# A window attention stage in a four-layer kernel: 128 + 64 channel rows, values per pixel through DRAM, a respread schedule

## The chip, the cores and the metric

The kernel runs as one program on one core of a Trainium2 chip. The core has five engines with a queue of instructions each: TensorE (PE in the profile; PEld is its weight load), VectorE (DVE), ScalarE (ACT), GpSimd (POOL) and SyncE (SP), which here only issues DMAs. Each works through its own queue in order, and semaphores hold an instruction back until what it needs is there. The metric is device time of one execution in microseconds (us), lower is better.

## The reference

Four layers follow each other on an image batch x of 4 x 192 x 64 x 64 in float32: a deformable convolution with channel attention (layer 0), a non-local block (layer 1), overlapping window attention with a gated MLP (layer 2), and a masked depthwise convolution (layer 3). Only the attention of layer 2 is concerned here:

```python
y = _conv1x1(_ln_c(x, n1g, n1b), qkv_w, qkv_b)          # 192 -> 576 channels, each pixel
cols = _unfold(y, WS, STRIDE, PAD)                      # 8x8 windows, step 6, 3 zeros around
L = cols.shape[-1]                                      # 11 x 11 windows
win = cols.reshape(B, 3 * HEADS, ch, WS * WS, L).transpose(0, 4, 1, 3, 2)
q = win[:, :, :HEADS] * temp[None, None]                # 6 heads of 32 channels
k = win[:, :, HEADS:2 * HEADS]
v = win[:, :, 2 * HEADS:]
attn = jnp.einsum('blhic,blhjc->blhij', q, k) + bias[None, None]
e = jnp.exp(attn - jnp.max(attn, axis=-1, keepdims=True))
s = jnp.sum(e, axis=-1, keepdims=True)
s_img = _reverse(s, H, W)                               # overlapping windows added up
o_img = _reverse(jnp.einsum('blhij,blhjc->blhic', e, v), H, W).reshape(B, HEADS, ch, H, W)
out = (o_img / s_img[:, :, None]).reshape(B, C, H, W)
```

Note that the unfolding comes after the projection: outside the image q, k and v are zero, and a pixel in the overlap of windows has one value vector that up to four windows use.

## The kernel before

The program goes over the four images. For each it runs `layer1`, beside which the gathers of the next image's layer 0 are woven, then `windows` (the attention of layer 2), then `rest` (the remainder of layer 2, layer 3, and the next image's first MLP). The constants of all layers are loaded and folded by `constants()`, whose steps are taken between those of the first image's gathers; there the gain and shift of layer 2's first layer norm go into the weights `qkvT`, and its mean is taken out of them.

`windows` goes over 11 rows of windows (`wr`). Channels lie as two halves of 96 partitions. Two sets of strips `xs`, `qs`, `ks` hold 8 image rows (with the zeros around) of normalized input, queries and keys; a window row brings 6 new ones, and `shared` copies the 2 rows that it has in common with the row before, on POOL. The 97th partition of `xs` is a row of ones, which adds the bias in the projection. For a window row there are these parts:

- `load` fetches the new input rows (SP, one DMA); `norm` is a generator that can be run up to a named step: squares on ACT (SQUARE), variances on PE, then square, difference and maximum, logarithm and exponential for the inverse root on ACT and DVE (VARIANCE, INVERSE), then its spread to all partitions on PE (L392) and the multiplication on DVE (L1122).
- `project_rows` makes queries and keys of one half: two projections of two matmuls (L1150, L1151). A float32 matmul shows in the profile as two passes.
- `queries` and `inputs` lay `qs` and `xs` out by window on POOL (`by_window`).
- The 11 windows are taken in three groups of four. `scores` makes the scores of a group on PE (L1185), adds the position bias, takes the maximum and subtracts it on DVE (L1191, L1197, L1198). `exponentials` takes the exponential on ACT (L1203) and the sums of it on DVE (L1205, L1209).
- `turned` takes a pair of windows: it makes their values on PE from the laid out input (L1225) and copies them out on ACT (L1230), transposes the exponentials on PE (L1233) and copies them into `et` on ACT (L1237). `outputs` multiplies both into a strip in PSUM (L1253, L1261).
- `collect` copies the finished strip out, `inverses` takes the inverse of the sums (ACT), and `finish` spreads it on PE (L1298) and multiplies on DVE (L1299).

The order of all this is written out by hand under `tc.manual_schedule()`: the loop over `wr`, `g` and `pair` at the end of `windows` is the order in which each engine gets its work. In it the scores of a group are made one group ahead. In the first group of a row, each pair is followed by the projections of one half of the next row. Norms are made two rows ahead: SQUARE at the start of group 0, up to INVERSE at the end of group 1 and ahead of that group's exponentials, and the spread and multiplication at the start of group 2, ahead of its pairs. At the end of row 1, `load_image` fetches the whole image for `rest` with 16 DMAs on SP.

PSUM tiles with the tag "a" (projections, values, transposes, `finish`) share two buffers; the score tile, the norms' tile and the output strip have one each.

## Time and profile before

| what | us |
| --- | --- |
| median of 3 runs | 6399.53 (6394.88 to 6402.87) |
| the profiled execution, its own time | 6392.29 |
| its span, first to last instruction | 6390.5 |
| up to the first `windows` (first image's layers 0 and 1) | 1480 |
| first `windows` (1480 to 1748) | 268, PE busy 245.96 |
| first `rest` (1748 to 2190) | 442, PE busy 382.11 |
| one steady row of windows (1569.28 to 1592.32) | 23.04: PE busy 21.25, DVE 14.54, ACT 15.13, POOL 6.63 |

The boundaries are read from the chain of waits: the last matmul of layer 1 (L1041) ends near 1480, the first of `rest` (L1496) starts at 1748; the later images' `windows` lie at 2990, 4507 and 5747.

A line of the profile names the line of the kernel, engine, operation, then out<-in by the program's names, shapes as partitions x elements, and how often. In a group, the numbers after the bar are busy us in all and mean ns of one, and behind the second bar the engine's idle time just before, with what ended it. In order of time, a line begins with the start and the duration in us, and a bracket gives the idle time before it and what it waited for. `SPq` is the issue of a DMA on SP's queue. PEclk is the granted clock of TensorE, 1.00 at full speed.

### The profile page before, as it was taken

The page shows a single profiled execution, that of the slowest core. Times are in us where ns is not written, and L with a number is a line of the kernel's source. Part 1 is how long each engine was busy: PE and PEld are TensorE (multiplying, and loading weights), DVE is VectorE, ACT ScalarE, POOL GpSimd, SP SyncE. Part 2 cuts the span into 40 slices and gives each one's busy share as a digit, 9 for nine tenths or more (in the row PEclk, how much of TensorE's full clock was granted, in tenths as well). Part 3 has the DMA queues.
Part 4 walks back from the last instruction along what each step waited for, and adds up shares of the span by engine and source line. Part 5 has one row for each costly group of instructions (what it writes and reads, how often), then busy time and mean ns, then how long its engine had stood idle before and what let it go on. Part 6 is the DMA issues. An engine that isn't in the chain of part 4 may idle for free.

```text
span 6390.5 us, 106371 instructions
## 1 busy us (share of the span) xinstructions
PE 5900.9 (92%) x40528; PEld 4039.0 (63%) x40528; DVE 4612.9 (72%) x6850; ACT 3779.2 (59%) x6552; POOL 2111.3 (33%) x2293
## 2 busy tenths in 40 slices
PE   7888999999989899999988899999998989999897
PEld 4455588886544568887654458888654457776543
DVE  3864199985677669996676839998567867765667
ACT  3764388875654358885654438887565536545542
POOL 2763077752200047772210017775220000003200
PEclk8989999999989999999999999999998999999998
DMA  6995267751010267772110057775111010001000
GB/s 193 308 316 152 81 195 223 224 178 37 24 29 17 74 200 221 226 222 69 35 36 24 21 145 227 222 223 171 36 27 29 21 57 11 13 15 38 5 7 22
DMA packets 330117, 698.60 MB, mean 109 GB/s; under 512 B 59894, under 2 KB 216838, under 8 KB 328839
## 3 DMA queue, kind: packets, MB, share of 16 engines
q0 software_dynamic: 92736, 455.22, 22.0%
q1 hardware_dynamic: 236038, 235.78, 13.5%
q8 instruction: 321, 5.26, 0.3%
q14 instruction: 190, 1.55, 0.1%
q10 hardware_dynamic: 832, 0.79, 0.0%
HBM read 611.25 MB, written 78.87 MB: 108 GB/s over the span
## 4 chain that ended last, share of the span: by engine, by line
PE 63%; DVE 20%; ACT 5%; DMA 5%; issue 4%; SPq 2%; POOL 1%; POOLq 0%; DVEq 0%; ACTq 0%
PE y L1041 11%; PE s L973 10%; PE h L650 7%; DVE ha L1403 2%; PE h L1595 2%; PE qk L1150 2%; PE v L1225 2%; PE o L878 2%; PE qk L1151 2%; DMA ring<-table,idx 2%; DVE ga L1403 2%; PE po L538 2%; DVE gate L1403 2%; DVE row L639 1%; DVE top L980 1%
## 5 line engine op out<-in xcount | busy, mean ns | idle before, releaser
L632 POOL DMA_INDIRECT ring<-table,idx x1152 | 1671.1, 1451 | 946.0 <-DVE row L639 172.7
L973 PE MATMUL s<-ths,ph 96*128 96x256 f32 x4096 | 982.5, 381 | 6.4 <-ACT sc L975 4.0
L973 PEld LDWEIGHTS s<-ths,ph 96*128 96x128 f32 x4096 | 776.6, 191 | 131.1 <-ACT sc L975 6.3
L638 ACT ACTIVATE row<-ring,pos 128x384 f32<-128x384 f32 x1152 | 673.0, 609 | 240.4 <-DVE xo L643 147.2
L639 DVE SCALAR_TENSOR_TENSOR row<-ring,fr,row 128x384 f32<-128x384 f32 x1152 | 673.1, 611 | 111.2 <-ACT row L638 106.3
L1041 PE MATMUL y<-sc,gx 128*97 128x256 f32 x3008 | 716.4, 379 | 0.0
L1041 PEld LDWEIGHTS y<-sc,gx 128*97 128x97 f32 x3008 | 489.3, 164 | 127.5 <-issue 5.1
L642 ACT ACTIVATE xo<-row,pos 128x192 f32<-128x192 f32 x1152 | 485.5, 448 | 64.2 <-PE h L650 32.2
L643 DVE SCALAR_TENSOR_TENSOR xo<-row,fr,xo 128x192 f32<-128x192 f32 x1152 | 445.4, 411 | 41.5 <-ACT xo L642 39.3
L975 ACT COPY sc<-s 128x1024 f32<-128x1024 f32 x376 | 377.1, 1003 | 157.0 <-PE s L973 154.2
L1038 DVE TENSOR_TENSOR sc<-sc,mbs 128x1024 f32<-128x1024 f32 x376 | 453.0, 1217 | 19.8 <-ACT mbs L999 19.7
L1039 ACT ACTIVATE sc<-sc 128x1024 f32<-128x1024 f32 x376 | 393.3, 1053 | 75.2 <-DVE sc L1038 72.1
L980 DVE TENSOR_TENSOR top<-top,sc 128x1024 f32<-128x1024 f32 x282 | 344.0, 1220 | 128.6 <-ACT sc L975 128.4
L650 PE MATMUL h<-ti,xo 128*128 128x192 f32 x2304 | 434.6, 327 | 0.0
L650 PEld LDWEIGHTS h<-ti,xo 128*128 128x128 f32 x2304 | 388.8, 190 | 28.8 <-issue 8.2
L1205 DVE TENSOR_REDUCE eh<-ex 128x12 f32<-128x768 f32 x132 | 125.4, 950 | 317.1 <-ACT ex L1203 317.1
L1403 DVE SCALAR_TENSOR_TENSOR ga<-gate,v,ga 128x1024 f32<-128x1024 f32 x234 | 300.3, 1283 | 6.7
L650 PE MATMUL h<-kept,xo 128*128 128x192 f32 x960 | 239.2, 381 | 70.5 <-DVE xo L643 62.0
L1645 POOL COPY gate<-gate 128x192 f32<-128x192 f32 x12 | 4.2, 348 | 904.9 <-ACT gate L1638 904.9
L650 PEld LDWEIGHTS h<-kept,xo 128*128 128x128 f32 x960 | 169.7, 210 | 162.9 <-DVE xo L643 116.4
L855 PE MATMUL h<-d_l0m,fc 128*128 128x256 f32 x768 | 217.5, 427 | 59.1 <-ACT z L1601 22.5
L1041 PE MATMUL y<-se,gx 128*97 128x256 f32 x1088 | 261.1, 380 | 0.5 <-ACT yn L1047 0.5
(402 smaller groups left out, 11090.8 us busy)
## 6 DMA issues: line engine op xcount, KB each, us to landing
ti<-table SPq DMA_DIRECT2D x768, 48.0 KB
ring<-table,idx POOLq DMA_INDIRECT x1152
xnd<-xn SPq DMA_DIRECT2D x4, 3270.0 KB
xi<-in_x_dram SPq DMA_DIRECT2D x32, 384.0 KB
xk<-xd SPq DMA_DIRECT2D x32, 384.0 KB
xd<-xc SPq DMA_DIRECT2D x64, 192.0 KB
table<-tt SPq DMA_DIRECT2D x32, 384.0 KB
xc<-xd SPq DMA_DIRECT2D x60, 192.0 KB
```

Of the source, the lines that this page charges most:

```text
L632: nc.gpsimd.indirect_dma_start(out=gt.rearrange("p q r c -> p (q r c)"), out_offset=None, in_=corners, in_offset=bass.IndirectOffsetOnAxis ...
L638: nc.scalar.activation(row, gt[:, 0], AF.Copy, scale=pos[:, t, 9 + tap : 10 + tap])
L639: nc.vector.scalar_tensor_tensor(row, gt[:, 1], fr[:, t, 9 + tap : 10 + tap], row, ALU.mult, ALU.add)
L642: nc.scalar.activation(xo[:, j, :], row[:, 0, :], AF.Copy, scale=pos[:, t, tap : tap + 1])
L643: nc.vector.scalar_tensor_tensor(xo[:, j, :], row[:, 1, :], fr[:, t, tap : tap + 1], xo[:, j, :], ALU.mult, ALU.add)
L650: nc.tensor.matmul(acc[m // 2][:, bass.ts(m % 2, C)], lhsT=xo.rearrange("p j c -> p (j c)")[:, bass.ts(m, 128)], rhs=tt, start=t == 0 and ...
L973: nc.tensor.matmul(p[:, t, :], lhsT=ph[:, bass.ts(G * g + t, 128)], rhs=ths[i], start=True, stop=True)
L980: nc.vector.tensor_tensor(tops[i], tops[i], to, ALU.max)
L1038: nc.vector.tensor_tensor(ex, ex, mbs[i].unsqueeze(1).to_broadcast([128, G, QN]), ALU.add)
L1039: nc.scalar.activation(ex, ex, AF.Exp)
L1041: nc.tensor.matmul(py, lhsT=gx[:, G * g + t, :], rhs=ex[:, t, :], start=g == 0 and t == 0, stop=g == NG - 1 and t == G - 1,)
L1403: nc.vector.scalar_tensor_tensor(acc[:, b], src(tap, b), w[:, tap : tap + 1], acc[:, b], ALU.mult, ALU.add)
```

## The change

All of it concerns layer 2's attention.

- **Channels** lie as 128 and 64, the second block filled with zeros up to 128. `qkvT` is laid out so that its columns are 128 of q, 128 of k, then the last 64 of q beside the last 64 of k, then v. A row so has three projections (`t` = 0, 1, 2) of two matmuls with 128 rows and columns, where it had four with 96. The ones row is gone: the bias of q and k (`qkb`) is added by ACT as it writes them out, and the second block of q and k is written in two pieces of 64 partitions.
- **Strips** are the image rows 6 x wr to 6 x wr + 5, normalized into `xz` without zeros around, and not kept over rows. `qs` and `ks` hold 9 rows and share 3; `xs`, `xw` and `inputs` are gone.
- **Values** are made once per pixel: `values` multiplies 128 pixels at a time (three tiles a row where there were six pairs of windows), DVE adds the bias `vb`, and two DMAs write them to `values_dram`. `fetch` reads them back by window with 16 DMAs of 8 partitions each into `vw`, which `outputs` uses. The zeros around are written once, by POOL's DMAs for the first image.
- **Order**: the first and third projection and the values stay in group 0, the second projection goes to group 1. DVE's sums (`summed`) are taken after the next scores' bias, ahead of maximum and subtraction (`lowered`); in group 0 these two come after the first value tiles. The norm's spread and multiplication go behind the first pair of group 2, SQUARE to the end of group 2 a row earlier.
- **Loads** are two DMAs (128 and 64 partitions) into two fixed buffers whose lower part of the second block is set to zero once.
- **Constants**: the weights are loaded raw into a temporary tile (one DMA more) and scaled into `qkvT`; `qkb` and `vb` come from a few small matmuls; there is one step more. The gain, shift and temperature are also laid out as 128 and 64.

The diff, cut to its core:

```diff
+    values_dram = dram.tile([SW, STRIDE * (NWIN + 1), C], F32, tag="values", name="values")
...
             def load(wr, by=nc.sync):
+                n, at = strip(wr)
+                t = given[wr] = xrs[wr % 2]
+                lo, hi = split(t, n)
+                by.dma_start(out=lo, in_=x_flat[b % 2][0:M, at : at + n])
+                by.dma_start(out=hi[half(0)], in_=x_flat[b % 2][M:C, at : at + n])
...
+            if b == 0:
+                blank = s1.tile([128, 3 * C], F32, tag="blank", name="blank")
+                nc.gpsimd.memset(blank, 0.0)
+                for r in (0, 1, 2, SW - 1):
+                    nc.gpsimd.dma_start(out=values_dram[r, 0:SW], in_=blank[0:SW, 0:C])
+                inner = values_dram[PAD : PAD + H]
+                nc.gpsimd.dma_start(out=inner[:, 0:PAD, :], in_=blank[0:H].rearrange("p (w c) -> p w c", c=C))
+                nc.gpsimd.dma_start(out=inner[:, PAD + W, :], in_=blank[0:H, 0:C])
...
+                xz = xzs[wr] = sb.tile([M, 2, STRIDE * W], F32, tag="xz", name=f"xz_{name}")
+                nc.vector.tensor_tensor(xz[:, :, 0:n], src[:, :, 0:n], pb.unsqueeze(1).to_broadcast([M, 2, n]), ALU.mult)
...
+            def project_rows(wr, t):
+                qs, ks = sets[wr % 2]
+                n = strip(wr)[0]
+                rows, chans = slice(PAD, PAD + n // W), bass.ts(t, M)
+                p = ps2.tile([128, 512], F32, tag="a", name=f"qk_{b}_{wr}_{t}")[:, :n]
+                for k, part in enumerate(split(xzs[wr], n)):
+                    nc.tensor.matmul(p, lhsT=qkvT[:, k, chans], rhs=part, start=k == 0, stop=k == 1)
+                p = p.rearrange("p (r c) -> p r c", c=W)
+                temp = VW["l2_temp"]
+                if t == 1:
+                    nc.scalar.activation(ks[:, 0, rows, inside], p, AF.Identity, bias=qkb[:, 1:2])
+                    return
+                of, k = (half(0), 1) if t else (slice(0, M), 0)
+                nc.scalar.activation(
+                    qs[of, k, rows, inside], p[of], AF.Identity, bias=qkb[of, t : t + 1], scale=temp[of, k]
+                )
+                if t == 2:
+                    nc.scalar.activation(ks[half(0), 1, rows, inside], p[half(1)], AF.Identity, bias=qkb[half(0), 3:4])
+
+            def values(wr, part):
+                n = strip(wr)[0]
+                parts = split(xzs[wr], n)
+                tiles = [i for i in (2 * part, 2 * part + 1) if 128 * i < n]
...
+                    for j, i in enumerate(tiles):
+                        for k, of in enumerate(parts):
+                            nc.tensor.matmul(
+                                p[:, j, :], lhsT=of[:, bass.ts(i, 128)], rhs=qkvT[:, k, 2 * C :],
+                                start=k == 0, stop=k == 1,
+                            )
+                    nc.vector.tensor_tensor(
+                        vs[:, tiles[0] : tiles[-1] + 1, :], p, vb.unsqueeze(1).to_broadcast([128, len(tiles), C]), ALU.add
+                    )
+                if part == 0:
+                    return
+                m, r = n // 128, PAD + STRIDE * wr
+                to = values_dram[r : r + 2 * m, inside, :].rearrange("(i h) c k -> h c i k", h=2)
+                for h in range(2):
+                    nc.sync.dma_start(out=to[h], in_=vs[half(h), 0:m, :])
+
+            def fetch(wr):
+                vw = vws[wr] = sb.tile([128, (NWIN + 1) // 2, C], F32, tag="vw", name=f"vw_{b}_{wr}")
+                for i in range(2):
+                    n = (NWIN + 1 - i) // 2
+                    for r in range(WS):
+                        row = values_dram[STRIDE * wr + r, STRIDE * i : STRIDE * i + 2 * STRIDE * n]
+                        at = 64 * i + WS * r
+                        nc.sync.dma_start(
+                            out=vw[at : at + WS, 0:n, :], in_=row.rearrange("(n c) k -> c n k", n=n)[0:WS]
+                        )
...
                 for wr in range(NWIN):
                     for g in range(groups):
                         nxt = (wr, g + 1) if g + 1 < groups else (wr + 1, 0)
-                        if 0 < wr < NWIN - 2 and g == 0:
-                            norm(wr + 2, SQUARE)
                         if nxt[0] < NWIN:
-                            sc = scores(*nxt)
+                            sc, top = scores(*nxt)
+                        sums = summed(wr, g, ex)
+                        if nxt[0] < NWIN and (g > 0 or wr + 1 == NWIN):
+                            lowered(*nxt, sc, top)
                         if wr + 3 < NWIN and g == 1:
                             load(wr + 3)
-                        if wr + 2 < NWIN and g == 2:
-                            norm(wr + 2)
                         for pair in range(WG // 2):
-                            ops = turned(wr, g, pair, ex)
+                            ops = turned(wr, g, pair, (ex, sums))
                             if due is not None:
                                 outputs(*due)
                                 if g == 0 and pair == 0:
                                     collect(wr - 1)
                             due = ops
-                            if g == 0 and wr + 1 < NWIN:
-                                project_rows(wr + 1, pair)
+                            if wr + 1 < NWIN:
+                                if g == 0:
+                                    project_rows(wr + 1, 2 * pair)
+                                    values(wr + 1, pair)
+                                if g == 1 and pair == 0:
+                                    project_rows(wr + 1, 1)
+                                if g == 0 and pair == 0:
+                                    lowered(*nxt, sc, top)
...
+                            if wr + 2 < NWIN and g == 2 and pair == 0:
+                                norm(wr + 2)
                         if wr + 2 < NWIN and g == 1:
                             norm(wr + 2, INVERSE)
                         if nxt[0] < NWIN:
                             ex = exponentials(*nxt, sc)
-                        if g == 0 and wr + 1 < NWIN:
-                            for i in (1, 2):
-                                shared(wr + 1, i)
-                            queries(wr + 1)
-                            inputs(wr + 1)
-                        if g == 2 and wr + 2 < NWIN:
-                            shared(wr + 2, 0)
+                        if wr + 3 < NWIN and g == 2:
+                            norm(wr + 3, SQUARE)
+                        if wr + 1 < NWIN:
+                            if g == 0:
+                                shared(wr + 1, 0)
+                                queries(wr + 1)
+                            if g == 1:
+                                shared(wr + 1, 1)
+                                fetch(wr + 1)
```

## The prediction

> **What bounds the kernel now.** I read the sums over stretches first, then one steady row in order of time, then groups of instructions. The change works in four stretches, one for each image, in which `windows` runs. In the fences the columns after the stretch are busy us (and instructions) of PE, PEld, DVE, ACT and POOL, the granted clock, the share and the rate of DMA.
>
> ```profile
> span 6390.5 us, 106371 instructions
> 1480.00:1748.00 268.00, 245.96 (x3772) 161.75 (x3771) 160.97 (x234) 166.93 (x354) 76.94 (x207) 0.98 0.11 30
> 2990.00:3259.00 269.00, 246.50 (x3773) 162.37 (x3772) 160.64 (x234) 167.00 (x354) 76.95 (x207) 0.98 0.11 29
> 4507.00:4776.00 269.00, 246.47 (x3775) 162.29 (x3774) 160.93 (x234) 167.08 (x354) 76.92 (x207) 0.98 0.11 30
> 5747.00:6018.00 271.00, 246.89 (x3771) 162.69 (x3770) 161.36 (x235) 167.04 (x354) 82.27 (x209) 0.97 0.09 25
> ```
>
> TensorE is busy 92% of them, the other engines 62% or less. So the order on PE and its pauses set the time: 1077 us of 6390.5, 17%, and nothing outside can gain. A steady row takes 23.05 us (scores of its second group start at 1569.28, then at 1592.32), its three groups 9.75, 4.78 and 8.53. From start to start on PE: scores 0.73 each, a projection of four passes 1.35, a value block 0.68, three transposes 0.43, one pair's outputs 0.48, variances 0.9, spread 0.72, `finish` 0.69. That is 3 x 0.73 + 4 x 1.35 + 6 x (0.68 + 0.43 + 0.48) + 0.9 + 0.72 + 2 x 0.69 = 20.1 us; 2.9 are pauses, the longest here:
>
> ```profile
> 1584.95 0.21 DVE L402 TENSOR_SCALAR r_l2n<-r_l2n 128x96 f32<-128x96 f32 x1
> 1585.19 0.37 ACT L363 ACTIVATE r_l2n<-r_l2n,eps 128x96 f32<-128x96 f32 x1 [0.57 <-DVE r_l2n L402]
> 1585.60 0.28 ACT L364 ACTIVATE r_l2n<-r_l2n 128x96 f32<-128x96 f32 x1
> 1585.79 0.83 ACT L1203 ACTIVATE ex<-ex 128x768 f32<-128x768 f32 x1
> 1585.94 0.92 PE L392 MATMUL pb_l2n<-r_l2n,spread 128*96 128x96 f32 x8 [1.34 <-ACT r_l2n L364]
> ```
>
> PE waits 1.34 us for the norm's root; the exponential of the next group stands behind that root on ACT.
>
> **What it removes on PE.** Three projections in place of four: 1.35. Three value tiles of 128 pixels in place of six window pairs: 3 x 0.68 = 2.04. Filling to 128 rows costs nothing there: the spacing goes with the columns, and those stay 384 and 192. PE's work falls to 16.75 us a row.
>
> **What moves on the others**, by these groups (mean ns after the comma; last, DVE's idle time):
>
> ```profile
> L1205 DVE TENSOR_REDUCE eh<-ex 128x12 f32<-128x768 f32 x25 | 23.7, 949 | 60.2 <-ACT ex L1203 60.2
> L1191 DVE TENSOR_TENSOR ex<-s,bias 128x768 f32<-128x768 f32 x25 | 23.7, 948 | 0.0
> L1203 ACT ACTIVATE ex<-ex 128x768 f32<-128x768 f32 x25 | 20.9, 836 | 0.1
> L1230 ACT COPY vs<-v 128x192 f32<-128x192 f32 x41 | 13.1, 319 | 22.6 <-PE v L1225 22.5
> L1299 DVE TENSOR_TENSOR oi<-ot,rb 96x384 f32<-96x384 f32 x16 | 8.8, 547 | 3.9 <-PE rb L1298 3.9
> ```
>
> ACT loses six value copies (1.9 us a row) and writes projections in four pieces as before. DVE gains the bias of the values, 0.55 and 0.35 (as L1299's shapes). POOL loses the gather of `xw` and the shared rows of `xs`, 2.7 us of 6.6, off the path. DVE's sums now come behind the next scores' bias, so its 2.4 us of idle time a row for ACT go; but sums stand ahead of maximum and subtraction: from scores to exponential is 0.95 + 0.95 + 0.25 + 0.95 + 0.97 = 4.1 us on DVE, not 2.9. A row has 14.54 us of DVE and 15.13 of ACT before, 15.4 and 13.2 after, both below PE.
>
> **The pauses of the new row**, walked by hand in the new order with these durations. Group 0: PE 7.3 us, nothing late. Group 1: the second half of the third projection is written on ACT ahead of the exponential, 0.65 of pause before the transposes; work 4.85. On ACT then come copies, the projection moved here (0.58, it waits for PE), two inverses (1.04), copies, square, root, and the exponential ends 8.65 us after the group's start. PE has finished the next scores at 6.2 and needs it for the transposes: a pause of 2.4 us. The spread, moved behind them, no longer fills it. Group 2: PE's second `finish` needs the buffer that DVE's multiplication frees, which is behind sums, maximum and subtraction: 0.5. Together 16.75 + 3.7 = 20.45 us.
>
> Such a pause has a second price. In one row of the second stretch:
>
> ```profile
> 3204.70:3208.20 3.50, 3.50 (x69) 2.86 (x61) 2.65 (x4) 3.00 (x7) 2.32 (x8) 1.00 0.00 0
> 3208.20:3211.60 3.40, 2.02 (x90) 1.77 (x80) 1.87 (x4) 2.76 (x7) 0.00 (x0) 1.00 0.18 48
> 3211.60:3215.00 3.40, 3.40 (x27) 2.64 (x26) 3.29 (x5) 1.27 (x3) 0.00 (x0) 0.51 0.00 0
> 2085.22 2.93 PE L855 MATMUL h<-d_l0m,fc 128*128 128x256 f32 x6 [2.46 <-ACT gl L869]
> 2085.20:2088.70 3.50, 3.48 (x10) 2.38 (x12) 3.39 (x4) 0.33 (x1) 0.00 (x0) 0.51 0.02 5
> ```
>
> Around a pause of 1.38 us PE was busy 2.02 of 3.4 us, the clock was then 0.51 for 3.4 us, and this group took 10.13 us, not 8.53: 1.6 for one fall. A pause of 2.46 in another stage did the same. Most rows stay just above that edge now; with 2.4 us most would fall. I take four rows in five at 1.6 (bounds: none, and every row for two such stretches, 2.9): +1.3, a row of 21.75.
>
> The Trainium skill ("TensorE: Matmul & The Clock Gate", "HAM oscillation — how this bites in real kernels") asks only that PE have no idle gap above about 3.4 us. By that rule no row would fall and the total would be some 40 us lower; the rows above fell at 1.38 and 2.46, and I go by them.
>
> **The way through DRAM.** A row now has 2 stores, 2 loads and 16 fetches on SP, which issued one load. No row shows the fetch; the nearest, 8 partitions with 8 pieces each, is L302:
>
> ```profile
> L302 SPq DMA_DIRECT2D bias<-shifted x48: 685/685/812, 177.8 to 212.2; - x48
> 2113.20 2.06 DMA xd<-xa
> 611.85 2.91 DMA xa<-in_x_dram
> ```
>
> It went every 0.73 us (182.34, 183.07 in the chain); the medians of SP's other issues run from 0.30 (L1080) to 0.69, which is the range; single ones took up to 1.35, at L2027. From issue to the waiter a store took 2.0, a load 2.5 to 2.9. After the values' last add at 7.85 us of the row: stores at 7.9 and 8.5, landed 10.6, last fetch issued 10.6 + 15 x 0.73 = 21.6, landed 24.1. The first outputs of the next row want it at 21.75 + 4.8 = 26.5: hidden by 2.4 us, until a fetch costs 0.9. Twice in a stretch it isn't hidden:
> - Start: the last add at 1497.5 gives a landing at 1513.7; PE is there at 1509.5. Pause 4.2, the load of row 2 behind it holds up ACT's square, and the clock falls again: +6.5 (bounds 2 and 9).
> - `load_image` issues 16 DMAs (some 9 us on SP), which now follow row 1's long fetches and stand ahead of row 2's stores:
>
> ```profile
> 1527.00:1541.00 14.00, 12.90 (x220) 8.78 (x219) 6.66 (x10) 9.82 (x22) 5.34 (x19) 1.00 0.93 238
> ```
>
> They fill the DMA engines for 14 us. Counted from row 1's start: image from 22.3, engines free at 37, stores landed 38.6, fetches 52; wanted at 2 x 21.75 + 4.8 = 48.3. Pause 3.7 and a fall, +4.9 (bounds 0 and 9).
>
> The skill's "DMA: Bandwidth & Descriptors" ("Measured") calls transfers under 64 KB descriptor-dominated; these have 30 to 36 KB. Its figure for 64 KB, 0.95 us, taken as the issue step, would add some 25 us in all, an estimate.
>
> **Once.** The fold of the weights has one DMA more, a few little matmuls and DVE steps; L302 shows that SP's order is on the path there. On POOL six fills of zeros (0.68 each, as POOL's loads at L1080) and two more loads, mostly where POOL idles. +3 (0 to 10).
>
> **Sum.** Per stretch: rows 1 to 8, 8 x -1.3 = -10.4; rows 9 and 10, without norms and without the long pause, walked the same way 17.6 and 13 for 20.1 and 16: -5.5; start +6.5; image +4.9: -4.5. Four stretches -18, once +3: -15. The profiled execution took 6392.29 (span 6390.5), so 6377; the median of the runs shown is 7.2 higher, so **6384 us**.
>
> **Rivals.**
> - All that PE loses is gained (pauses stay 2.9, no falls): rows of 19.7, 8 x -3.35 = -26.8 in place of -10.4, total -81: 6319. For: PE is the bound by share. Against: DVE's longer way and ACT's order above.
> - Slower: each pause in group 2 costs two stretches of half clock (2.9). Rows then take 23.35, +0.3 x 8 in place of -10.4: total +33 to +40, 6437. It decides once a row loses over 2.6 us. For: after 1498.1 the clock stayed low for 10 us. Against: PE has work for 3.4 us after the pause.
> - Slower by SP: a fetch of 1.05 us makes the row 10.6 + 15.75 + 2.5 - 4.8 = 24.05; with start and image about +92, 6490. It decides from 0.98 us a fetch. Against: only single issues took as long.
>
> **How the numbers follow.** Forecast 0.45 (its own range 6350 to 6415), first rival 0.18, half clock 0.25, SP 0.08, something else 0.04. A measurement tells about 0.2%, 13 us. Faster: 0.25 of the forecast and the first rival, 0.43. Same: 0.17 of the forecast and the middle of the others, 0.23. Slower 0.34. Range 6300 to 6450: part of the first rival and the SP case stay out.
>
> **What would show it.** Right: PE's busy time in the stretches down by about 36 us each, transposes (L1233 of before) waiting 2.4 us for the exponential in group 2, clock 0.5 after many of them, rows near 21.7, pauses of some 4 us on outputs in rows 0 and 3 that a DMA of `vw` ends. Wrong: a fetch far from 0.73 us, rows near 19.7, or every row waiting for `vw`.

## The result and the profile after

The changed kernel took 6435.39 us (median of four runs, 6427.42 to 6444.96); the kernel before, beside it, 6397.20 (6393.62 to 6402.87). The ratio is 1.0055, with a 95% interval of 1.0039 to 1.0072: slower by 38 us, where the forecast was 15 us below the times shown. In a second comparison the ratio was 1.0038 (1.0022 to 1.0054).

From the page of the changed kernel: span, busy time by engine, and the group of transposes that answers to L1233 of before.

```profile
span 6431.4 us, 105494 instructions
PE 5832.6 (91%) x39860; PEld 4021.8 (63%) x39860; DVE 4645.4 (72%) x6899; ACT 3717.7 (58%) x6288; POOL 1979.4 (31%) x1989
...
L1325 PE MATMUL t<-ident,ex 128*128 128x128 f32 x792 | 156.6, 313 | 151.3 <-ACT ex L1300 151.3
```

PE issues 668 matmuls fewer and is busy 68 us less, and yet the span is 41 us longer. The last line says where PE stood: 151 us ahead of transposes, all of it waiting for the exponential on ACT. The four stretches, from the first filler matmul of `windows` to the first matmul behind it (columns as in the prediction):

```profile
1495.50:1764.30 268.80, 218.18 (x3594) 150.20 (x3593) 168.22 (x244) 151.82 (x288) 56.52 (x143) 0.92 0.26 65
3017.60:3296.90 279.30, 229.00 (x3593) 156.75 (x3593) 168.01 (x244) 151.82 (x288) 52.75 (x136) 0.87 0.24 61
4546.50:4822.70 276.20, 225.95 (x3594) 154.69 (x3593) 168.50 (x244) 151.90 (x288) 52.79 (x136) 0.88 0.24 62
5800.30:6065.10 264.80, 220.01 (x3544) 152.41 (x3543) 167.53 (x240) 149.33 (x285) 50.86 (x128) 0.89 0.23 59
```

Cut the same way, the stretches of before take 268.3, 269.3, 268.6 and 264.5. So the stretches give +18.5 us of the 41, at a clock of 0.87 to 0.92 where before had 0.97 to 0.98. The other 22.5 lie outside: the first gather ends 20.8 us later.

A steady row in order of time, start and duration in us, the pause of group 2 (the instructions of ACT and DVE that decide it, and PE's next):

```profile
3225.38 0.52 ACT L1384 ACTIVATE rs<-ot 6x384 f32<-6x384 f32 x1
3225.93 0.52 ACT L1385 ACTIVATE rs<-rs 6x384 f32<-6x384 f32 x1
3226.16 0.80 PE L1279 MATMUL s<-ks,qw 32*64 32x64 f32 x48
3226.46 0.97 ACT L1329 COPY et<-t 64x384 f32<-64x384 f32 x2
3227.45 0.25 ACT L435 ACTIVATE r_l2n<-pv_l2n 128x96 f32<-128x96 f32 x1
3227.73 0.26 DVE L436 TENSOR_TENSOR r_l2n<-pv_l2n,r_l2n 128x96 f32<-128x96 f32 x1 [2.35 <-ACT r_l2n L435]
3228.27 0.38 ACT L398 ACTIVATE r_l2n<-r_l2n,eps 128x96 f32<-128x96 f32 x1 [0.57 <-DVE r_l2n L437]
3228.68 0.28 ACT L399 ACTIVATE r_l2n<-r_l2n 128x96 f32<-128x96 f32 x1
3228.87 0.83 ACT L1300 ACTIVATE ex<-ex 128x768 f32<-128x768 f32 x1
3229.75 0.47 PE L1325 MATMUL t<-ident,ex 128*128 128x128 f32 x1 [2.80 <-ACT ex L1300]
```

The scores of the next group are done at 3226.96, and PE's next work is the transposes at 3229.75. The exponential they need was lowered on DVE by 3225.4, but stands on ACT behind the inverses, two copies and the root. The sums over stretches of 3.4 us around that pause:

```profile
3222.50:3225.90 3.40, 3.40 (x71) 2.33 (x71) 2.82 (x4) 2.07 (x4) 0.00 (x0) 1.00 0.69 172
3225.90:3229.30 3.40, 1.05 (x63) 0.77 (x54) 1.33 (x3) 2.72 (x7) 0.00 (x0) 1.00 0.39 104
3229.30:3232.70 3.40, 2.95 (x21) 1.80 (x22) 2.90 (x4) 1.35 (x3) 0.00 (x0) 0.50 0.11 28
3232.70:3236.10 3.40, 3.40 (x28) 2.67 (x26) 1.56 (x3) 0.69 (x2) 0.00 (x0) 0.50 0.00 0
3236.10:3239.60 3.50, 3.50 (x72) 2.09 (x70) 2.31 (x3) 2.28 (x5) 0.00 (x0) 1.00 0.02 5
```

PE is busy 1.05 of 3.4 us, and the granted clock is then 0.50 for two such stretches. Rows (from the scores of one row's third group to those of the next) take 21.1 us where the clock did not fall, 22.5 with one stretch at half clock and 23.7 to 23.9 with two. In these four stretches the clock falls 11, 14, 12 and 11 times; before it was 1, 2, 1 and 2.

### The profile page after: what moved, and what is told of

Same layout as the page of the kernel before. It is cut to its first block, busy times and chain, and to the rows that moved or that the text cites. A ratio compares the mean times of both kernels' runs of the same rounds, so it can differ in the third digit from the quotient of the medians.

```text
span 6431.4 us, 105494 instructions
## 1 busy us (share of the span) xinstructions
PE 5832.6 (91%) x39860; PEld 4021.8 (63%) x39860; DVE 4645.4 (72%) x6899; ACT 3717.7 (58%) x6288; POOL 1979.4 (31%) x1989
## 3 DMA queue, kind: packets, MB, share of 16 engines
q0 software_dynamic: 93264, 455.82, 21.9%
## 4 chain that ended last, share of the span: by engine, by line
PE 62%; DVE 19%; ACT 8%; DMA 5%; issue 4%; SPq 1%; POOL 1%; DVEq 0%; ACTq 0%; POOLq 0%
PE y L1076 11%; PE s L1008 10%; PE h L685 6%; PE qk L1203 3%; PE po L573 2%; PE h L1699 2%; DVE ha L1507 2%; DMA ring<-table,idx 2%; PE o L913 2%; DVE ga L1507 2%; PE t L1325 2%; DVE row L674 2%; DVE gate L1507 1%; PE o L1345 1%; DVE top L1015 1%
## 5 line engine op out<-in xcount | busy, mean ns | idle before, releaser
L1329 ACT COPY et<-t 64x384 f32<-64x384 f32 x484 | 231.4, 478 | 253.7 <-PE t L1325 248.7
L1325 PE MATMUL t<-ident,ex 128*128 128x128 f32 x792 | 156.6, 313 | 151.3 <-ACT ex L1300 151.3
L890 PE MATMUL h<-d_l0m,fc 128*128 128x256 f32 x768 | 213.3, 420 | 59.1 <-ACT z L1705 22.5
```

## The experiments

They were made in four sittings, in which the kernel before took 6394 to 6579 us, so each ratio is to its runs in the same sitting. The sum of the four stretches comes from each profile; "start" runs from the first filler to the first scores in stretches 1 to 3. A single stretch of the same kernel can differ by 10 us between two profiles (the changed kernel's first: 268.8 and 278.4), so small differences in the sums say little.

| run | ratio to before (95%) | four stretches, us | start, us | steady rows, us |
|---|---|---|---|---|
| before, twice | 1; 1.0012 (0.9994 to 1.0030) | 1071; 1071 | 18.0; 18.2 | 23.05 |
| changed, twice | 1.0055; 1.0038 | 1089; 1092 | 31.2 | 21.1 to 23.9 |
| x_warm | 0.9932 (0.9904 to 0.9960) | 1033 | 31.1 | 21.03 |
| x_spread | 0.9943 (0.9922 to 0.9963) | 1033 | 30.8 | 20.4, some 22 to 23.3 |
| x_exp | 0.9884 (0.9851 to 0.9917) | 1006 | 31.2 | 19.98 |
| x_expinv | 0.9863 (0.9828 to 0.9898) | 998 | 31.1 | 19.88 |
| x_load | 0.9990 (0.9965 to 1.0015) | 1071 | 19.4 | 21.1 to 23.9 |
| x_raw | 1.0022 (1.0003 to 1.0041) | 1087 | 30.4 | 21.1 to 23.9 |
| x_best2 | 0.9773 (0.9747 to 0.9800) | 930 | 19.4 | 18.76 |
| x_fetch2 | 1.1813 (1.1775 to 1.1852) | 2268 | 31.2 | 48 |
| x_fetchd | 1.0224 (1.0200 to 1.0248) | 1210 | 24.6 | 22.5 to 25.4 |
| b_spread | 1.0018 (0.9993 to 1.0043) | 1095 | 18.2 | 23.1, 24.7 |
| b_exp | 1.0039 (1.0018 to 1.0060) | 1102 | 18.1 | 23.2, 24.6 |
| b_best | 1.0018 (1.0007 to 1.0030) | 1079 | 18.2 | 23.17 |

**x_warm: the pause filled.**

```diff
                             sc, top = scores(*nxt)
+                        if wr + 2 < NWIN and g == 2:
+                            keep_warm(pvs[wr + 2][:, 256:512], 4)
```

> The changed kernel with four matmuls of 256 columns into an unused part of the variances' bank (an estimate from the 0.73 us that 384 columns take: 4 x 0.49 = 1.95 us) put on PE between the scores and the transposes of group 2, where PE now stands still for 2.8 us. It adds work and takes no wait away. Theory 'clock': the pause costs little itself beyond its 2.8 us; what makes rows differ (21.1 us without a fall, 22.5 with one stretch at half clock, 23.9 with two) are the falls after it. With the fillers the clock stays at 1.0 in rows 3 to 8 and every row takes 21.1: per stretch -6, -14, -12.5, -12.5, in all -45, some 6390 us. Rival 'chain': rows are set by the way from scores to exponential on DVE and ACT, PE's slower clock lies beside it, and the fillers gain under 10 us: 6425 to 6435.

Work was added, and the stretches became 56 to 59 us shorter than those of the changed kernel's two profiles, where 45 were expected. All rows from the third to the eighth take 21.03 us. The same place in the row:

```profile
3321.80:3325.20 3.40, 2.20 (x100) 1.78 (x98) 1.06 (x2) 2.80 (x6) 0.00 (x0) 1.00 0.16 43
3325.20:3328.60 3.40, 3.37 (x29) 2.60 (x30) 2.78 (x5) 2.29 (x5) 0.00 (x0) 1.00 0.37 96
3328.60:3332.00 3.40, 3.40 (x78) 2.34 (x76) 2.80 (x5) 1.22 (x2) 0.00 (x0) 1.00 0.01 4
```

The fillers themselves waited 1.24 us for the reader of their bank, and a pause of that length leaves PE busy 2.2 of 3.4 us: the clock stays at 1.00. "Clock" holds, "chain" falls: the half clock after the pause, not the pause alone, makes rows long.

**x_spread: one part of the change undone.** The spread of the root goes back ahead of the pairs.

```diff
+                        if wr + 2 < NWIN and g == 2:
+                            norm(wr + 2)
                         for pair in range(WG // 2):
...
-                            if wr + 2 < NWIN and g == 2 and pair == 0:
-                                norm(wr + 2)
```

> The changed kernel with only the spread of the norm's root put back ahead of the pairs of group 2, where it was before the change. PE then waits for the root itself, 2.1 us after the scores by the trace, runs the spread (1.1 us) and has the exponential ready right after it. Theory 'cover': the later place of the spread is a loss of the change by itself, about 0.7 us a row in work that no longer fills the pause, and the falls with it, since a pause of 2.1 us with more work around it makes the clock fall less: rows of 20.2 to 20.5 without a fall, some falls left, ratio 0.990 to 0.998. Rival 'same pause': the clock falls as before and the spread only changes places with the transposes, rows of 22.5 to 23.9, ratio 1.002 to 1.007.

"Cover" holds: 56 to 59 us less in the stretches than with the spread later, ratio 0.9943. In a row of it:

```profile
3285.42 0.80 PE L1279 MATMUL s<-ks,qw 32*64 32x64 f32 x48
3287.94 0.28 ACT L399 ACTIVATE r_l2n<-r_l2n 128x96 f32<-128x96 f32 x1
3288.13 0.83 ACT L1300 ACTIVATE ex<-ex 128x768 f32<-128x768 f32 x1
3288.27 2.02 PE L427 MATMUL pb_l2n<-r_l2n,spread 128*128 128x96 f32 x8 [2.05 <-ACT r_l2n L399]
3290.09 0.85 PE L1325 MATMUL t<-ident,ex 128*128 128x128 f32 x3
```

PE starts again 2.05 us after the scores, and the spread covers the exponential. This row still fell (the spread takes 2.02 us at half clock); most others did not and took 20.4. With the exponential where the change left it on ACT, undoing the later place of the spread is enough to turn the loss into a gain. It is not the only way: x_warm and x_exp keep that place and gain as well.

**x_exp and x_expinv: the order on ACT.**

```diff
+                        if nxt[0] < NWIN:
+                            ex = exponentials(*nxt, sc)
                         if wr + 2 < NWIN and g == 1:
                             norm(wr + 2, INVERSE)
-                        if nxt[0] < NWIN:
-                            ex = exponentials(*nxt, sc)
```

In x_expinv, `inverses(wr - 1)` also goes from the first pair of group 1 to behind that exponential.

> The changed kernel with the exponential of the next scores put ahead of the norm's root (the last step of the norm in group 1) on ACT; nothing else moves. In the trace ACT is ready with the copies 1.3 us before the exponential starts, and its scores are lowered on DVE 3.4 us before. Theory 'order on ACT': the pause of 2.8 us in group 2 shrinks to 1.5, which lies at the length that mostly did not make the clock fall before: rows of 19.8 to 20.5, 26 rows with some 2.5 us less, 6360 to 6375 us. Rival 'DVE': the exponential waits for the lowering on DVE, so moving it gains under 0.3 us a row: 6425 to 6435.

> As the kernel before this one, and the two inverses (0.52 us each) of the finished row also moved behind the exponential on ACT. Theory 'order on ACT': the pause shrinks to about 0.5 us, no falls, rows of 18.8 to 19.5: 6320 to 6345 us. Rival 'late root': the norm's root and the inverses then end some 2.3 us after the exponential, and PE waits for them at the finish or the spread of group 2 instead, so that the row is no shorter than with the exponential alone moved: 6360 to 6375.

The same place in a row of x_exp:

```profile
3240.51 0.96 DVE L1296 TENSOR_TENSOR ex<-ex,mx 128x768 f32<-128x768 f32 x1
3243.54 0.84 ACT L1300 ACTIVATE ex<-ex 128x768 f32<-128x768 f32 x1
3244.44 0.55 PE L1325 MATMUL t<-ident,ex 128*128 128x128 f32 x3 [1.39 <-ACT ex L1300]
```

The exponential was held up by its place on ACT, not by DVE: the pause is 1.39 us for 2.80, rows take 19.98 (19.8 to 20.5 was expected), the steady ones without a fall, and the stretches are 83 to 86 us shorter. The ratio of 0.9884 is a larger gain than the 0.994 to 0.997 that 6360 to 6375 us would be. Moving the inverses too gave 0.1 us a row where 0.5 to 1.2 were expected. The root then ended later, and the spread waited 0.65 us for it: "late root" holds.

**x_load: the start.**

```diff
-                xr = s1.tile([M, 2, STRIDE * W], F32, tag=f"xr{j}", name=f"xr{j}_{b}")
+                xr = sb.tile([M, 2, STRIDE * W], F32, tag="xr", name=f"xr{j}_{b}")
                 nc.gpsimd.memset(xr[half(1), 1, :], 0.0)
                 xrs.append(xr)
-            load(0, nc.gpsimd)
-            load(1, nc.gpsimd)
+                load(j, nc.gpsimd)
```

> The changed kernel with the two tiles of loaded rows taken from the first pool, where they lay before the change, and each tile's zeros and load in turn. In the trace of the changed kernel the zero fill of the first tile waits on POOL until 1504.08 for the store of the last attention result, and the two first loads stand behind it; before, the load was there at 1480. Theory 'place in memory': the tile shares its memory with the stored tile; without that the first row's variances start at about 1501 in place of 1507.6, each start of the stretch is 5 to 7 us shorter, -20 to -28 in all: 6407 to 6415 us. Rival 'values first': the start is long because all values and projections of row 0 now come ahead of the first scores at half clock, and the load is not what sets it: under 8 us, 6427 to 6435.

The start of the changed kernel, in order of time:

```profile
1501.73 0.31 SPq L1050 DMA_DIRECT2D xd<-xc  x1
1504.08 0.77 POOL L1124 MEMSET xr<- 64x384 f32 x2 [86.92 <-DMA xd<-xc]
1504.80 0.59 POOL L1118 DMA_DIRECT2D xr<-xd  x1
1507.61 1.03 PE L1170 MATMUL pv_l2n<-xr,mean_all 128*32 128x96 f32 x16 [6.43 <-DMA xr<-xd]
...
1510.79 3.43 DVE L437 TENSOR_SCALAR r_l2n<-r_l2n 128x96 f32<-128x96 f32 x1
...
1513.64 0.51 POOL L1154 MEMSET rs<- 128x512 f32 x1
...
1514.26 0.37 ACT L398 ACTIVATE r_l2n<-r_l2n,eps 128x96 f32<-128x96 f32 x1 [3.79 <-DVE r_l2n L437]
```

The zero fill waits for the store of `xc`, the load stands behind it, and PE stands still for 6.43 us. With the tile in the other pool:

```profile
1583.02 0.85 ACT L1161 ACTIVATE sq_l2n<-xr 128x768 f32<-128x768 f32 x1
1588.19 0.54 PE L1168 MATMUL pv_l2n<-xr,mean_all 128*32 128x96 f32 x16
1589.70 0.92 DVE L437 TENSOR_SCALAR r_l2n<-r_l2n 128x96 f32<-128x96 f32 x1
1601.97 0.80 PE L1277 MATMUL s<-ks,qw 32*64 32x64 f32 x48
```

The first row is there at once, and a start takes 19.4 us for 31.2: twice what was expected: a step of 3.43 us on DVE also shrinks to 0.92, and the clock stays at 1.00. Against 18.0 before, a start is still 1.4 us longer, with values and projections ahead of the scores. "Place in memory" holds for three stretches. The four together became only 18 to 21 us shorter, the low end of what was expected: rows 1 to 8 took 181.7 us for 178.2 and 178.8 in the changed kernel's two profiles, with more rows of 23.9, and the fourth stretch gained nothing at its start (19.1 for 19.8; 12.2 before). There no store holds up the load; L437 takes 5.51 us in x_load and 5.55 in the changed kernel where its like took 0.91 before. The ratio of 0.999 is below the 1.002 to 1.003 that 6407 to 6415 us would be; the stretches explain about half of what this run gains on the changed kernel, the rest was not followed.

**r_before, r_after and x_raw: outside the stretches.** x_raw releases the raw weights of the fold only after the tables of relative positions are loaded:

```diff
-        raws.close()
...
+        raws.close()
         v48 = late("v48", a["v48"])
```

> The kernel before, unchanged, profiled on the chip on which the next runs are made, so that the stages outside the four stretches can be set against each other on one chip. Both theories expect a ratio of 1.000; the stage up to the first normed rows (551.4 us in the first profile) may differ by tens of us from chip to chip.

> The changed kernel, unchanged, on the same chip. Of the 41 us between the two first profiles 19 lie in the four stretches and 22 outside, nearly all of these before 572 us (20.8 there). Theory 'fold': the outside part belongs to the change (the longer fold of the weights ahead of the chain of little DMAs on SP), and the end of the first gather is again 15 to 21 us later than in the kernel before on this chip. Rival 'chip': it is scatter of the gather, and the end of the first gather differs by less than 8 us either way.

> The changed kernel with the raw weights of the fold held until after the tables of relative positions are loaded; only the place in memory of the tile 'shifted' changes. In the trace of the changed kernel the first DMA of 'shifted' starts on SP at 175.30 us, when the last matmuls of the fold have read the raw weights whose place it takes; before it started at 168.19. Theory 'fold blocks SP': the chain of 48 little DMAs and the load of xi behind it start at 163 to 166 us in place of 175 and the first gather ends 8 to 14 us earlier than in the unchanged kernel: 6420 to 6428 us by the first chip's numbers. Rival 'work': the gather is late because of more work on PE and DVE in the fold, and the earlier DMAs gain under 4 us.

The last matmul of the first gather starts at 550.5 and 571.3 us in the first two profiles, at 607.4 and 612.4 in the second two: +20.8 and +5.0. The second is the rival's "less than 8", so most of the 20.8 is not shown to belong to the change. In x_raw the first DMA of `shifted` starts at 169.6 for 176.5 (163 to 166 was expected) and the gather's last matmul at 604.1 for 612.4: 8.3 us earlier, the low end of "fold blocks SP"; in x_best2, which has this edit too, at 606.7. The ratios 1.0022 and 1.0038 have overlapping intervals. The other profiles show how far such numbers scatter, since the edits inside `windows` do not touch this gather. With the constants of before it ends at 609.3 and 616.6 (b_spread, b_exp), in the same sitting with those of the change at 614.6 and 617.3 (x_spread, x_fetch2); in the last sitting at 559.3 (b_best) and 565.2 (x_fetchd). So in three sittings the change costs 3 to 6 us here, one kernel differs by up to 7 from profile to profile, and x_raw's 8.3 is hardly more than that.

**x_fetch2 and x_fetchd: are the fetches hidden?** Each fetch twice, first into the same tile, then into one that nobody reads:

```diff
-                        nc.sync.dma_start(
-                            out=vw[at : at + WS, 0:n, :], ...
+                        for t in (vw, vx):
+                            nc.sync.dma_start(
+                                out=t[at : at + WS, 0:n, :], ...
```

> The changed kernel with every fetch of the values issued twice (32 DMAs on SP a row in place of 16, the same data). In the trace 16 fetches are issued in 5.6 to 8.2 us, 0.35 to 0.5 us each, not the 0.73 that the prediction took from another shape; in steady rows they are issued some 9 us ahead of the first outputs that need them, in row 0 about 1 us ahead. Theory 'hidden': steady rows keep their length, only the first outputs of a stretch wait, by 5 to 7 us: +20 to +28 us, ratio 1.008 to 1.010. Rival 'SP bounds': every row waits for its values with 6 to 8 us more, over +100 us, ratio 1.02 or more.

> The changed kernel with every fetch issued a second time into a tile of its own that nobody reads: 16 DMAs more a row on SP (5.6 to 8.2 us by the trace) and twice the data, no wait between the two. Theory 'hidden': steady rows keep their 21.1 to 23.9 us, since 16 fetches are issued some 9 us ahead of the outputs that need them; only the first outputs of a stretch, which had about 1 us to spare, wait 5 to 7 us more: +20 to +30 us, ratio 1.007 to 1.011. Rival 'SP bounds': all rows become longer by 2 us or more, +70 us, ratio 1.015 or more.

x_fetch2 measured something else. What SP waited for, and who waited for the tile (us, times):

```profile
  DMA vw<-values: 1313.8, 51
...
  PE o L1346: 1112.8, 44
```

The second copy of each fetch waited for the landing of the first, since both write the same place. It shows what values cost that are late in every row (25 us a row), not what 16 issues cost. In x_fetchd, with no such wait, 32 issues take 15 us a row for 6.2, and steady rows from the fifth to the eighth stay at 22.5 to 25.4, within 2 us of the changed kernel's: hidden there. But row 0 takes 23 to 26 us for about 19, and row 2, with the image's load in it, 30 to 34 for 21 to 23. The ratio is twice what was expected and the stretches grew by about 120 us where 20 to 30 were expected: by these numbers alone the rival (1.015 or more, +70 us) would hold. Its mechanism does not, since it wanted every row longer: from the fifth to the eighth, four rows take 94.2 us on average for 93.7. What grew is row 0 (by 6 us), row 2 (by 10) and rows 9 and 10 with the end (by 6), and the way to row 0's third group (by 5), although the first scores came 6.6 us earlier, which says that the extra tile also moved others in memory. "Hidden" holds for steady rows alone.

**b_spread, b_exp and b_best: the same order in the kernel before.**

```diff
 b_spread: norm(wr + 2) behind finish(wr - 1, pair) of the first pair of group 2
 b_exp:    also exponentials(*nxt, sc) ahead of norm(wr + 2, INVERSE)
 b_best:   also inverses(wr - 1) at the end of group 0
```

> The kernel before with one part of the change alone: the spread of the root after the first pair of group 2 in place of ahead of the pairs. There a value block of 0.68 us still stands between scores and transposes, and the exponential is ready 0.7 us after the root. Theory 'cover': PE's pause only goes from the spread (1.34 us) to the transposes (about 1.4), rows stay within 0.3 us of 23.05, ratio 0.999 to 1.003. Rival 'falls': the clock, which in rows of before just held, now falls in most rows: rows of 24.5, ratio 1.005 to 1.007.

> The kernel before with the spread after the first pair and the exponential ahead of the norm's root, as in the changed kernel with that order. Tells what the order on ACT is worth without the new layout. Theory 'order on ACT': the exponential is ready at 1585.56 for 1586.62, the pause of PE before the transposes shrinks from 1.3 to 0.3 us, the root is still in time for the spread behind them: rows of 21.9 to 22.3, 8 a stretch, some -30 us, ratio 0.994 to 0.996; the rest of what the changed kernel with this order gains over before (rows of 20.0) is then the new layout's. Rival: the root is late for the spread by as much as the exponential was, rows of 22.9 to 23.1, ratio 0.999 to 1.001.

> The kernel before with the whole mended order: the exponential ahead of the norm's root, the inverses at the end of group 0, the spread after the first pair. Theory 'layout': the kernel before has 20.1 us of PE work a row and 2.9 of pauses, so the order can give at most some 1.5 us a row; rows of 21.6 to 22.6, ratio 0.990 to 0.997, well short of the 0.977 of the changed kernel with that order. Rival 'order': the gain is the order's alone, rows of 20.1 to 20.8, ratio 0.980 to 0.985. A third: the clock falls in it as in the run with the exponential alone, rows of 23 to 24.6, ratio 1.000 to 1.005.

None is faster. b_spread's ratio is inside its expectation, but rows alternate between 23.1 and 24.7, so the falls of the rival are there as well. b_exp and b_best missed: rows of 23.2 without a fall and, in b_exp, every other one 24.6 with one, where 21.9 to 22.3 and 21.6 to 22.6 were expected. b_best's ratio is that of its third theory, but its steady rows hardly fall. Its trace shows why they do not shrink either:

```profile
3140.42 0.30 ACT L1230 COPY vs<-v 128x192 f32<-128x192 f32 x1
3140.78 0.89 PE L1298 MATMUL rb<-rs,headsel 128*96 128x384 f32 x2 [1.42 <-ACT vs L1230]
```

The pause has only moved. `finish` needs a buffer of tag "a", which is free when ACT has copied a pair's values out, and that copy now stands behind the root on ACT: 5.7 us of such waits in four rows, where before PE waited 5.3 for the root itself. The new layout has no such copies. So the order alone is worth nothing in the old layout.

**x_best2: put together.** x_load, x_raw and x_exp, with `inverses(wr - 1)` at the end of group 0.

> Changes put together: loaded rows in the first pool, the exponential ahead of the norm's root, the two inverses already at the end of group 0 on ACT, the raw weights held. With the exponential ahead, moving the inverses behind it had given only 0.1 us a row (19.88 for 19.98), because the root came later and the spread waited 0.65 us for it. Theory 'late root': with the inverses in group 0, where ACT stood idle for 0.7 us, neither waits: rows of 18.9 to 19.4, and starts of 19.4 us in place of 31.1: stretches 30 to 36 us shorter than before, ratio 0.972 to 0.982. Rival 'group 0': the inverses there delay the copies and with them the outputs of group 1, rows stay at 19.7 to 20.0 and stretches end 24 to 28 us shorter than before, ratio 0.983 to 0.988.

Rows of 18.76 us, below what was expected, and 0.9773 of before (6405.62 us for 6556.31): faster than both kernels. Its stretches:

```profile
1587.00:1821.50 234.50, 210.59 (x3593) 145.12 (x3593) 163.04 (x244) 151.41 (x288) 51.42 (x135) 0.96 0.29 74
3098.20:3329.10 230.90, 207.38 (x3593) 142.00 (x3593) 162.81 (x244) 151.20 (x288) 47.74 (x128) 0.97 0.28 74
4608.60:4838.70 230.10, 205.24 (x3593) 141.11 (x3592) 162.78 (x244) 151.18 (x288) 47.69 (x128) 0.99 0.28 74
5814.50:6049.30 234.80, 204.43 (x3550) 140.78 (x3542) 165.64 (x241) 148.83 (x285) 51.31 (x127) 0.95 0.26 67
```

With the clock at 0.95 to 0.99 PE is busy 36 to 41 us less a stretch than in the profile of before in the same sitting (241.9 to 247.8), and the stretches are 29 to 39 us shorter. The layout's gain is real; the order and the tile's place had hidden it. The order gains only with the layout (b_best).

## Why the prediction was wrong

It forecast -15 us for the profiled execution, and +41 came. By its terms, in us for one stretch (mean of four, from the first two profiles):

| term | predicted | measured |
|---|---|---|
| start, to the scores of row 0's third group | +6.5 | +10.4 (31.4 to 41.8) |
| rows 1 to 8 and the image's stall | -10.4 + 4.9 | -3.8 (182.0 to 178.2) |
| rows 9 and 10, end | -5.5 | -1.9 (54.3 to 52.4) |
| four stretches | -18 | +18.5 |
| once, outside | +3 | +22.5 |

Of the 56 us between forecast and result, about 20 lie outside, 16 in the starts, 14 in rows 9 and 10 with the end, and 7 in rows 1 to 8 with the image. The step that failed in its mechanism is the start, which was taken for a wait on values. In rows 1 to 8 the pauses were dearer than forecast, but the image's stall did not come, and most of the miss cancels: that term came near its number by luck.

- **PE's work** was right: 36 us less a stretch was forecast, 36 to 41 show in x_best2, where the clock hides little.
- **The pause in group 2** was right in place and cause and near in size: 2.4 us forecast, 2.8 measured, on the exponential behind copies, inverses and root. x_exp and x_spread show both causes.
- **The price of the pause** was set too low: "I take four rows in five at 1.6". One stretch at half clock costs 1.4 us (21.1 to 22.5), but in later rows of a stretch two follow each other and cost 2.8. That was the second rival's mechanism, and steady rows of 23.7 to 23.9 are its 23.35. Its 6437 meets the measured time only because misses elsewhere cancel. Without falls eight rows take 164.7 us (x_warm); the walk gave 8 x 20.45 = 163.6 (its three pauses, 0.65, 2.4 and 0.5, add up to 3.55, not to the 3.7 in the sum, so it was 20.3 a row). The falls cost 178.2 - 164.7 = 13.5 us a stretch for 10.4.
- **What the rows were held against** failed as well: the gain was counted from eight rows of 23.05, 184.4 us, but the first two rows of before take 20.5 and 22.5 (24.9 in the fourth stretch), and the eight take 182.0. That alone is 2.4 us a stretch that could not be gained.
- **The start** was taken for a wait on values, 4.2 us on the first outputs. They did not wait: the 16 fetches were issued in 6 us. The loss was the first row's load behind a zero fill in reused memory, +13 us to the first scores in three stretches, and x_load takes away 11.8. The prediction had read the loads' order on POOL and not where the tile lies. It also put POOL's fills at nothing for DVE; L437 stretches beside them, and in the fourth stretch, whose start grew by 7.7 us, that step alone took 4.6 more.
- **Fetch and image**: the step "0.73 us each", from another shape, was too dear. The median issue in the changed kernel:

```profile
L1253 SPq DMA_DIRECT2D vw<-values x704: 263/301/1679, 1527.3 to 6040.1; - x176
```

With what lies between issues that is 0.35 to 0.5 us. The stall of 4.9 us after the image's load did not come: row 2 takes 21.1 to 22.6 us, as its neighbours do; x_fetchd shows that little was missing. That SP would not bound steady rows was right. Its side estimate of 25 us for issues of 0.95 us counts steady rows alone; by its own chain start and image would move by 3.3 us each in every stretch, as much again.
- **Rows 9 and 10** were walked with hand-summed work and without the end of the stretch: rows of 20.8 and 16.6 came for 17.6 and 13. x_best2 has 17.2 and 14.1, so pauses seem to make most of the difference.
- **Once**: +3 with bounds of 0 and 10; 20.8 came in the first gather of the first pair of profiles, 5.0 in the second, 3 to 6 in two later sittings. So the term was about right for the gather, and most of the 20.8 belongs to that pair; what made it stays open. Outside the gather, the changed kernel's clock fell in the projection of the second image's stage (its `phi` matmuls take 47.4 us for 39.8 from first to last), and in that of the third in both kernels of the first pair, but only in the changed one of the second. In b_spread and b_best, which have the old layout, the second image's fell too (47.3 and 47.4 us), so it is not tied to the layout; it was not followed.

The Trainium skill's rule of 3.4 us ("TensorE: Matmul & The Clock Gate", "HAM oscillation — how this bites in real kernels") would have let no row fall. Pauses of 2.8 us fell in most rows here, and the measurement decides.

## What to carry to other kernels

A pause of PE has two prices: its length, and the half clock after it, which here cost half as much or as much again; so work that stood in a pause is not free to move, and before moving it one asks what PE does there instead. On an engine that works in order, put what the busiest engine waits for ahead of what is needed later. A tile that moves to another pool inherits the waits of whatever lay there before, and a load behind its zero fill inherits them too.

## What the runs showed of the hardware

- **Fillers make a kernel faster.** Four matmuls of 256 columns whose results nobody reads, 2 us a row, made the stretches 56 to 59 us shorter, by keeping the granted clock at 1.00 in rows that had 0.50 for 3.4 or 6.8 us.
- **The same pause may or may not cost.** In the first two stretches of the changed kernel pauses of 2.79 us were followed by no fall (rows of 21.1), one or two stretches at half clock. All changes of the clock in its trace lie whole multiples of 3.413 us apart, as on a fixed grid, and where the pause lies on that grid goes with what follows:

```profile
1584.08:1587.49 3.41, 1.74 (x96) 1.46 (x85) 1.01 (x4) 2.73 (x7) 0.00 (x0) 1.00 0.42 105
1587.49:1590.90 3.41, 2.29 (x27) 1.66 (x28) 2.72 (x5) 1.99 (x5) 0.00 (x0) 1.00 0.31 68
1590.90:1594.32 3.42, 3.37 (x80) 2.15 (x81) 3.02 (x5) 1.95 (x3) 0.00 (x0) 1.00 0.00 0
```

  Here the pause (1585.82 to 1588.61) is shared by two slots of the grid and the clock stays up. The pause at 3226.95 lies in one (PE busy 1.06 of 3.41 us), and two at half clock follow. In the four stretches of eight profiles (before, changed, x_warm, x_exp, x_load, x_best2, b_spread, b_exp) every one of 187 falls came after a slot with PE busy under 0.66 of it; but 105 of 1946 slots that kept the full clock lay under that too, so the busy share alone does not settle it.
- **DVE beside fills on POOL.** The step L437 (128x96) takes 0.21 us in a steady row and 3.43 in the start above, where it ends at 1514.22, with the last of POOL's fills (1513.64 + 0.51). In the four starts it took 3.43, 2.71, 3.34 and 5.55 us, each time to within 0.1 us of the end of a train of fills; in x_load 0.92 in three, where it ended with the first fill although more followed, and 5.51 in the fourth. The Trainium skill ("SBUF — State Buffer", "SBUF: two separate sides") tells of an exclusive lock on a port pair that the two engines share, held for one instruction. Here the wait went on over several fills in some starts and over one in others; no run varied them one by one, and what decides between the two is open.
